# A graph layer on one core: the table of turned rows made in the set-up, and more chunks taken from it

## The chip, the cores and the metric

One Trainium2 chip, one of its cores. The time is device microseconds for one launch of the kernel; the median over runs counts. A profile is of one execution, and its span is the time between the first and last instruction on the engines. The engines are called PE (TensorE), DVE (VectorE), ACT (ScalarE), POOL (GpSimd) and SP (SyncE, which here mainly starts DMAs).

## The reference, cut to what matters

12500 nodes with 128 features each, and 200000 edges sorted by their target `dst`.

```python
h   = jnp.maximum(_layernorm(x, axis=-1), 0.0)
agg = jax.ops.segment_sum(h[src], dst, num_segments=12500)
deg = jax.ops.segment_sum(ones, dst, num_segments=12500)
agg = agg / jnp.maximum(deg, 1.0)[:, None]
t = jax.nn.relu(agg @ Wg + h @ Ws + bg)      # 128 -> 128
t = jnp.tanh(t @ W1 + b1)                    # 128 -> 512
t = jnp.tanh(t @ W2 + b2)                    # 512 -> 512
out = x + t @ W3 + b3                        # 512 -> 128
```

## The kernel before, in words

**Set-up.** The first 123 us. The rows of x come in 11 pieces of up to ten tiles of 128 nodes (the loop at L300). Each piece is normalised by `centre` (DVE, with a square on ACT), `factors` (a square root on ACT) and `scale` (DVE), and the result `h` is stored in a DRAM table `htab`, one row of 512 bytes for each node (L317). The indices are loaded and turned by `indices`. Meanwhile POOL gathers the source rows of 80 "raw" chunks straight from x (L179), which are normalised later.

**Chunks.** The 200000 edges make 1563 chunks of 128. For each chunk the 128 source rows have to be in SBUF, one edge to a partition; `add` (L643) multiplies them on PE with a one-hot matrix of the targets and adds to a PSUM tile of the node block (`agg`, or `edge` for chunks that reach over a block's border). The rows of a chunk come in one of these ways:

- POOL gathers them with one indirect DMA from `htab` (`gather`, L386), into a ring of 24 buffers (`AHEAD`). This is the usual way, 1323 chunks before.
- Lane 0: SP starts 128 DMAs of one row each, with addresses from registers (`row_loads`, L415).
- Lane 1: ACT copies 128 columns, one by one, out of `tab` (`column_copies`, L436). `tab` is the whole of `h` turned, features on the partitions and nodes along the free axis, and lies in SBUF. The column's place is in a register.
- Lane 2: DVE does the same two columns at a time (`column_pairs`, L446).

Columns have to be turned back: `turn` (L456) does that on PE, with one product for an ACT chunk and two for a DVE chunk, into a PSUM tile `pm`, and ACT copies it to SBUF as `turned`. The places come into registers with loads of 16 on ACT and DVE and of 32 on SP (`offsets`, L395; the loads are L399).

**Who gets which chunk.** `slots` (L126) is every fourth chunk from `FROM` on, without raw ones. A loop with debts (`owed`) deals the slots to the lanes in the proportions of `SHARES`, which counts the chunks of lanes 0, 1 and 2: 14, 50 and 96. What is left goes to POOL.

**Layers.** When the chunks of a block of 512 nodes are through, the five layer parts follow (`part0` to `part4`): products on PE, activations on ACT (L473), a last addition on DVE (L805), a store by SP. `part0` reads `tab` as well, for `h @ Ws`.

**Order.** PE, ACT and SP run in the order in which the program is written (`keep_in_program_order`; the classes `pe` and `act` and the function `sp_dma`). The main loop (L882) goes through the chunks: it issues gathers up to 24 ahead, lets the lanes' generators go on at times that `load_times` (L833) has worked out in advance, issues the turns nine gathered chunks ahead, and puts layer parts between the chunks by a planner's costs (1.251 us for each gathered chunk).

**The table.** `tab` is made while the first chunks run: `own` (L693) loads a block of `htab` back, 25 loads in all, and `own_turned` (L701) turns it on PE (98 transposes into `pt`) and has ACT copy it to `tab` (25 copies). The calls stand ahead of the main loop and at L941, one block to every second chunk. Columns can be taken only when the table is there; the first slot is above chunk 104.

Of the kernel before, what the change touches and what calls it, by code (L numbers as in the profile page):

```python
# [22 lines left out]
F32 = mybir.dt.float32  # L23
# [8 lines left out]
P = 128  # L32
EPS = 1e-5
CPR = 16
BLK = 512
# [9 lines left out]
SPREAD = 8  # L45
EVERY = 4
AT = 3
SHARES = 14, 50, 96
FROM, UNTIL = 104, 1540
SBUFS = 4  # L50
MARGIN = 18
TOGETHER = 4
# [25 lines left out]
def windowed(ctx, tc, x, src, dst, Wg, Ws, bg, W1, b1, W2, b2, W3, b3, out, flag):  # L78
    nc = tc.nc
    N, D = x.shape  # L80
# [18 lines left out]
    def raw(c):  # L99
        return RAW0 <= c < RAW1 and (c - RAW0) % STEP < GRP  # L100
# [23 lines left out]

    lanes = ([], [], [])
    slots = [c for c in range(AT, NCH, EVERY) if FROM <= c < UNTIL and not raw(c)]  # L126
    owed = [0.5 * n for n in SHARES] + [0.5 * (len(slots) - sum(SHARES))]
    for c in slots:
        owed = [o + n for o, n in zip(owed, [*SHARES, len(slots) - sum(SHARES)])]
        kind = max(range(4), key=lambda k: owed[k])  # L130
        owed[kind] -= len(slots)
        if kind < 3:
            lanes[kind].append(c)
    apart = sum(lanes, [])

    blocks, n = [], 0
# [16 lines left out]
    ps_t = ctx.enter_context(tc.tile_pool(name="ps_t", bufs=1, space=PSUM))  # L153
# [22 lines left out]
    for g in range(NRAW):  # L176
        t = raws.tile([P, GRP, D], F32, name=f"raw{g}")
# [7 lines left out]
    ident = const.tile([P, P], F32, name="ident")  # L185
# [5 lines left out]
    lane = shared[:, :W_MAX]  # L191
# [8 lines left out]
    htab = dram.tile([NP, D], F32, name="htab")  # L200
    bytes_at = dram.tile([ahead_of + NROW * ROW + past_end], U8, name="bytes_at")
    tab = const.tile([P, NP], F32, name="tab")
# [33 lines left out]
    def factors(stats):  # L236
        nc.scalar.activation(stats[:, 1], stats[:, 1], AF.Sqrt, bias=eps, scale=1.0 / D)
        nc.vector.reciprocal(stats[:, 1], stats[:, 1])

    def scale(h, xt, k, stats):  # L240
        nc.vector.scalar_tensor_tensor(h, xt, 0.0, spread(stats[:, 1], k), op0=ALU.max, op1=ALU.mult)  # L241

    with tc.tile_pool(name="ln", bufs=2) as ln:
# [53 lines left out]


        pieces = [(0, 4), (4, PIECE - 4)] + [(t, min(PIECE, NT - t)) for t in range(PIECE, NT, PIECE)]
        for i, (t0, k) in enumerate(pieces):  # L300
            xt = ln.tile([P, PIECE, D], F32, name="xt", bufs=3)
            whole = min(N - t0 * P, k * P) // P
            rest = min(N - t0 * P, k * P) - whole * P
            if rest:
                nc.vector.memset(xt[:, whole, :], 0.0)
            nc.sync.dma_start(xt[:, :whole, :], x[t0 * P : (t0 + whole) * P, :].rearrange("(t p) d -> p t d", p=P))
            if rest:
                nc.sync.dma_start(xt[:rest, whole, :], x[(t0 + whole) * P : N, :])
            if i == 1:
                indices("src", src, 0, keep_src)  # L310
            stats = ps_a.tile([P, BLK], F32, name="agg")[:, : 2 * k].rearrange("p (s t) -> p s t", s=2)
            xt = xt[:, :k]
            centre(ln, xt, k, stats)
            factors(stats)
            h = ln.tile([P, PIECE, D], F32, name="h", bufs=2)
            scale(h[:, :k], xt, k, stats)
            nc.sync.dma_start(htab[t0 * P : (t0 + k) * P, :].rearrange("(t p) d -> p t d", p=P), h[:, :k])  # L317


        number = sp.tile([NROW, CPR], F32, name="number")  # L320
# [50 lines left out]
    ml = ctx.enter_context(tc.tile_pool(name="ml", bufs=2))  # L371
# [11 lines left out]
    def sp_dma(*a):  # L383
        tc.keep_in_program_order(nc.sync.dma_start(*a))
# [93 lines left out]
    def raw_stats(i):  # L478
        return stats_raw[:, :, i * GRP : (i + 1) * GRP]

    def raw_scaled(i):
        h = raw_rows[i]
        scale(h, h, GRP, raw_stats(i))
        for j in range(GRP):
            rows_t[RAW0 + i * STEP + j] = h[:, j]
# [202 lines left out]
                s = out  # L688
            nc.vector.tensor_tensor(out, s, rd[:, a0 - n : a1 - n], op=ALU.mult)  # L689

    owns, xss, stores = {}, {}, []

    def own(s):  # L693

        n0 = s * BLK
        k = -(-min(BLK, N - n0) // P)
        hb = ml.tile([P, BLK // P, D], F32, name="xb")
        sp_dma(hb[:, :k], htab[n0 : n0 + k * P, :].rearrange("(t p) d -> p t d", p=P))
        owns[s] = hb

    def own_turned(s):  # L701

        k = -(-min(BLK, N - s * BLK) // P)
        hb = owns.pop(s)
        pt = ps_t.tile([P, BLK // P, P], F32, name="pt")
        for t in range(k):
            pe.transpose(pt[:, t, :], hb[:, t, :], ident)
        act.copy(tab[:, s * BLK : s * BLK + k * P], pt[:, :k, :].rearrange("p t n -> p (t n)"))

    def own_part(b):  # L710

# [121 lines left out]
    def load_times(lane):  # L833
        use = [sum(o < c for o in order) for c in lanes[lane]]
        if not use:
            return
        step = (use[-1] - use[0]) // max(1, len(use) - 1)
        use = [max(FROM - 46 + MARGIN, use[0] - step), *use] if lane else [use[0] - step * k for k in range(SBUFS - 1, 0, -1)] + use
        if lane == 0:
            use = [max(u, FROM // 2 + 7 * step // 8 * i) for i, u in enumerate(use)]  # L840
        some = LOADS[2] if lane == 2 else TOGETHER
        for i in range(len(lanes[lane])):
            for k in range(P // some):
                yield max(1, use[i] + (use[i + 1] - use[i]) * k * some // P - (0, MARGIN, MARGIN + GRP)[lane])
# [9 lines left out]
    def store(upto):  # L854
        while stores and stores[0][0] <= upto:
            sp_dma(*stores.pop(0)[1:])
# [11 lines left out]
            if w[1] is None:  # L868
                work.remove(w)

    nown = -(-N // BLK)
    own(0)
    own(1)
    own_turned(0)
    own(2)
    onehot(0)
    onehot(1)
    told_begins()
# [3 lines left out]
    for c in range(NCH):  # L882
        g = c // GRP
        at = c
        store(c if c >= QUICK else c - LATE)
        if c % GRP == 0 and g + 2 < ngrp:
            onehot(g + 2)
            if raw((g + 2) * GRP):
                raw_scaled(((g + 2) * GRP - RAW0) // STEP)
            if g == 2 + NRAW + 2:  # L890
                worst = checked()
            if 2 <= g < 2 + NRAW:
                centre(ed, raw_rows[g - 2], GRP, raw_stats(g - 2), bufs=1)
            if g == 2 + NRAW + 5:
                factors(stats_raw)

        if c % (GRP // 2) == 0 and g + 2 < ngrp:
            copies, times = loading[2]
            while times and times[0] <= behind:
                times.pop(0)  # L900
                next(copies, 0)
        while c % GRP == GRP // 2 and counted < len(blocks) and reach[counted][-1] // GRP <= g + (c >= QUICK):
            count(counted)
            counted += 1
        while nxt < len(order) and nxt < behind + AHEAD:
            gather(order[nxt])
            nxt += 1
        if not raw(c) and c not in apart:
            behind += 1
            for rows_of_lane, times in loading[:2]:  # L910
                while times and times[0] <= behind:
                    times.pop(0)
                    next(rows_of_lane, 0)
            while turns and turns[0][0] <= behind:
                turn(turns.pop(0)[1])
        if c >= QUICK:

            there = 7.5 + 1.251 * (NRAW * GRP + order.index(c)) if c not in apart else 0
            if c == QUICK:
                now = there - SPREAD  # L920
            while soonest() and max(now, soonest()[2]) < there:
                go_on(soonest())
            now = max(now, there) + 0.27
        add(c)

        lead = LEAD if c < QUICK else 2
        if done < len(blocks) and (c - lead if across[done] else c) >= reach[done][-1]:
            quick = reach[done][-1] + LEAD >= QUICK

            prev, older = (i if i >= 0 and reach[i][-1] + LEAD < QUICK else None for i in (done - 1, done - 2))  # L930
            older = None if quick and prev is None else older
            work.append([layers(done, prev, older), 0, 0, 0, quick and blocks[done][1] <= P])
            done += 1

        if c % TILE_EVERY == 1 and c // TILE_EVERY < NT:
            tallied(c // TILE_EVERY)
            if c // TILE_EVERY == NT - 1:
                outside(worst)
            if c // TILE_EVERY + EARLY < NT:
                seen(c // TILE_EVERY + EARLY)  # L940
        if c % 2 == 1 and c // 2 + 1 < nown:  # L941
            own_turned(c // 2 + 1)
            if c // 2 + 3 < nown:
                own(c // 2 + 3)
        if c < QUICK:
            if c % 2 == 0:
                go_on(work[0] if work else None)
        if c == QUICK:
            for b, (_, n) in enumerate(blocks):
                if n < BLK:  # L950
                    own_part(b)
# [376 lines left out]
```

## Time and profile before

| what | before |
|---|---|
| median of three runs | 2171.02 us |
| lowest, highest | 2165.9, 2172.37 us |
| profiled execution | 2164.96 us |
| its span | 2163.2 us |
| granted PE clock, mean of the span | 0.75 |
| HBM read, written | 123.71 MB, 13.03 MB |

How to read a profile row: a group of instructions is given as line, engine, operation, output <- inputs (partitions x elements), xcount, then the busy time in us, the mean duration of one in ns, and after the bar the idle time of the engine just before these instructions, with what ended most of it. "issue" is idle time in which the engine waited for nothing that the profile shows, "remote" time that ended by an event whose sender isn't shown. Durations of neighbours on one engine may overlap, so busy time can be less than count times mean. Rows that begin with a line and have three numbers with slashes give the minimum, median and maximum duration in ns, and the first and last start. Rows that begin with two numbers are of the timeline: start and length in us. A row that begins with a window gives the busy time of PE, its weight loads, DVE, ACT and POOL in it, then the granted clock, the share of the DMA engines' time, and GB/s. The line PEclk gives the granted clock of PE in 40 slices, in tenths. SPq, ACTq and DVEq are the sequencers of these engines, which do the register loads and issue DMAs.

### The profile page before, as it was taken

To read this page: it belongs to the slowest core of one execution; us is meant where nothing else is said; L and a number is where in the kernel's file an instruction comes from. 1 tells how busy PE (TensorE), PEld (TensorE's weight loads), DVE (VectorE), ACT (ScalarE), POOL (GpSimd) and SP (SyncE) were. 2 spreads that over 40 slices of the span, in tenths; PEclk is the share of its full clock that TensorE was granted. 3 is DMA by queue.
4 is the path that set the end of the run, shared out by engine and by line. 5 is a ranking of instruction groups with operands and counts; after the bars stand their busy time and mean duration, and the time that the engine had idled before them with its cause. 6 is when DMAs were issued, how large, how long until landed. Compare 5 with 4: busy or idle time off the path is not lost.

```text
span 2163.2 us, 34925 instructions
## 1 busy us (share of the span) xinstructions
PE 1474.7 (68%) x5402; PEld 981.4 (45%) x5402; DVE 1274.1 (59%) x7014; ACT 933.4 (43%) x6907; POOL 1335.4 (62%) x1411
## 2 busy tenths in 40 slices
PE   0025543768687787776885876767787687798587
PEld 0024433445454454454553544545454454454457
DVE  3854365756466675665673765666576476566530
ACT  1201144545544444454544445445454454545432
POOL 7756666566666666666666566666666666666661
PEclk9999985766866766776676776777766776788589
DMA  5934221222221222222222122122222122221210
GB/s 137 243 99 124 58 51 49 52 54 58 54 58 49 61 59 55 54 61 59 52 59 57 49 59 58 51 59 60 51 57 63 47 61 66 53 61 53 56 48 22
DMA packets 132962, 139.16 MB, mean 64 GB/s; under 512 B 31655, under 2 KB 109347, under 8 KB 132536
## 3 DMA queue, kind: packets, MB, share of 16 engines
q0 software_dynamic: 44896, 92.04, 16.7%
q1 hardware_dynamic: 84558, 41.29, 7.1%
q10 hardware_dynamic: 3276, 3.51, 0.6%
q14 instruction: 181, 1.48, 0.2%
q8 instruction: 51, 0.84, 0.2%
HBM read 123.71 MB, written 13.03 MB: 63 GB/s over the span
## 4 chain that ended last, share of the span: by engine, by line
PE 37%; DVE 20%; issue 17%; another core or an unknown queue 11%; ACT 9%; DVEq 2%; DMA 1%; ACTq 1%; SPq 0%
PE pm L378 24%; DVE cols L451 12%; PE agg L378 7%; ACT cols L442 7%; PE edge L378 3%; DVEq L399 2%; ACT h L473 2%; PE pt L381 1%; DVE nearby L535 1%; ACTq L399 1%; PE pm L381 1%; DVE mT L689 1%; DVE oh L495 1%; DVE h L241 1%
## 5 line engine op out<-in xcount | busy, mean ns | idle before, releaser
L388 POOL DMA_INDIRECT rows<-htab,scol x1323 | 1257.7, 951 | 759.7 <-issue 294.0
L451 DVE SCALAR_TENSOR_TENSOR cols<-first_only,tab 128x2 f32<-128x2 f32 x6144 | 913.8, 217 | 404.8 <-issue 394.7
L378 PE MATMUL pm<-h,w 128*128 128x512 f32 (+4 forms) x1344 | 836.1, 724 | 184.1 <-ACT h L473 66.8
L442 ACT COPY cols<-tab 128x1 f32 x6400 | 713.9, 188 | 489.1 <-issue 482.3
L378 PEld LDWEIGHTS agg<-oh,rows 128*128 128x128 f32 x1914 | 420.2, 275 | 285.1 <-issue 269.9
L378 PE MATMUL agg<-oh,rows 128*128 128x24 f32 x1914 | 382.1, 314 | 38.7 <-issue 35.0
L378 PEld LDWEIGHTS pm<-h,w 128*128 128x128 f32 x1344 | 253.7, 237 | 213.7 <-ACT h L473 71.6
L378 PEld LDWEIGHTS edge<-oh,rows 128*128 128x128 f32 x732 | 138.7, 238 | 96.1 <-issue 91.1
L473 ACT ACTIVATE h<-pm,b2c 128x512 f32<-128x512 f32 (+4 forms) x112 | 70.7, 631 | 173.7 <-PE pm L378 57.7
L378 PE MATMUL edge<-oh,rows 128*128 128x24 f32 x732 | 131.3, 286 | 17.6 <-issue 14.0
L805 DVE TENSOR_TENSOR o<-pt,xb 128x512 f32<-128x512 f32 x23 | 15.9, 692 | 203.9 <-remote 83.2
L495 DVE TENSOR_TENSOR oh<-shared,dloc 128x192 f32<-128x192 f32 x186 | 64.8, 350 | 86.2 <-remote 34.1
L473 ACT ACTIVATE h<-pm,b1c 128x512 f32<-128x512 f32 (+4 forms) x112 | 70.1, 631 | 99.5 <-remote 33.6
L476 ACT COPY turned<-pm 128x128 f32<-128x128 f32 x146 | 38.2, 262 | 158.2 <-PE agg L378 60.6
L378 PE MATMUL pm<-ident,cols 128*128 128x128 f32 x192 | 57.9, 394 | 54.8 <-ACT h L473 27.3
L179 POOL DMA_INDIRECT raw<-in_x_dram,rsrc x80 | 76.8, 960 | 25.6 <-issue 24.1
L535 DVE TENSOR_SCALAR_CACHE_REDUCE nearby<-nearby,parity 128x656 uint8<-128x656 uint8 x98 | 87.0, 887 | 6.1 <-issue 6.1
L285 PE MATMUL pm<-ident,idx_f 98*128 98x98 f32 x32 | 6.2, 376 | 108.4 <-DVE idx_f L279 68.5
L378 PEld LDWEIGHTS pm<-ident,cols 128*128 128x128 f32 x192 | 40.9, 257 | 71.3 <-ACT h L473 33.8
L378 PEld LDWEIGHTS agg<-oh,turned 128*128 128x128 f32 x194 | 47.2, 270 | 55.9 <-issue 35.0
L381 PE MATMUL pt<-ident,xb 128*128 128x128 f32 x98 | 27.1, 431 | 61.0 <-issue 32.8
L381 PE MATMUL pm<-ident,degs 128*128 128x128 f32 x99 | 24.9, 374 | 62.9 <-ACT h L473 30.3
(120 smaller groups left out, 808.3 us busy)
## 6 DMA issues: line engine op xcount, KB each, us to landing
srows<-htab SPq DMA_DIRECT2D x1792, 0.5 KB
rows<-htab,scol POOLq DMA_INDIRECT x1323
nearby<-bytes_at SPq DMA_DIRECT2D x98, 82.0 KB
xb<-htab SPq DMA_DIRECT2D x24, 256.0 KB
xb<-in_x_dram SPq DMA_DIRECT2D x23, 256.0 KB
out_dram<-o SPq DMA_DIRECT2D x23, 256.0 KB
xt<-in_x_dram SPq DMA_DIRECT2D x8, 640.0 KB
htab<-h SPq DMA_DIRECT2D x8, 640.0 KB
```

The costliest lines, as they stand in the source:

```text
L179: nc.gpsimd.indirect_dma_start(out=t[:, j, :], out_offset=None, in_=x, in_offset=bass.IndirectOffsetOnAxis(ap=rsrc[:, g, j : j + 1], axis=0),)
L241: nc.vector.scalar_tensor_tensor(h, xt, 0.0, spread(stats[:, 1], k), op0=ALU.max, op1=ALU.mult)
L378: tc.keep_in_program_order(nc.tensor.matmul(*a, **k))
L381: tc.keep_in_program_order(nc.tensor.transpose(*a, **k))
L388: nc.gpsimd.indirect_dma_start(out=r, out_offset=None, in_=htab, in_offset=bass.IndirectOffsetOnAxis(ap=scol[:, c : c + 1], axis=0),)
L399: loads, vs = nc.values_load_multi_w_load_instructions(places[min(lane, 1)][r : r + 1, q // EVERY, p0 : p0 + LOADS[lane]], engines=[kind], ...
L442: tc.keep_in_program_order(nc.scalar.copy(to[:, t : t + 1], of))
L451: last[:] = [tc.keep_in_program_order(nc.vector.scalar_tensor_tensor(to, first_only, a, b.to_broadcast([P, 2]), op0=ALU.mult, op1=ALU.add))]
L473: tc.keep_in_program_order(nc.scalar.activation(*a, **k))
L476: tc.keep_in_program_order(nc.scalar.copy(*a))
L495: newest[:] = [nc.vector.tensor_tensor(oh[:, :k, :w], lane[:, None, :w].to_broadcast([P, k, w]), dloc[:, g * GRP : g * GRP + k][:, :, None ...
L535: done = nc.vector.tensor_scalar(w, w, parity[:, t % 2 : t % 2 + 1], None, op0=ALU.is_equal, op1=ALU.add, accum_out=found[:, t : t + 1])
```

## The change

The table is no longer made from reloaded rows. A new `turned(h, t0, k)` in the set-up turns a normalised piece, up to four tiles at a time, on PE and copies it to `tab` on ACT; it is called for a piece after the `factors` of the next one, and after the loop for the last. `own`, `own_turned` and their calls are gone. Slots begin at chunk 27 (`FROM` = 24); lane 0 still begins after 104 (`ROWS_FROM`). The lanes get 24, 100 and 100 chunks, and the dealing loop uses shares in fractions, with lane 0's share over the later slots only. `load_times` begins lanes 1 and 2 one step ahead of their first use, with no lower bound from `FROM`; lane 0's bound uses `ROWS_FROM`, which leaves its value as it was.

By instruction, from the two built programs: ACT column copies 6400 to 12800, their register loads 400 to 800; DVE pairs 6144 to 6400, loads 768 to 800; SP row DMAs 1792 to 3072, loads 56 to 96, reloads of `htab` 25 to 0; gathers from `htab` 1323 to 1259; `turned` copies 146 to 200; `tab` copies 25 to 29.

```diff
@@ -45,8 +45,8 @@
 SPREAD = 8
 EVERY = 4
 AT = 3
-SHARES = 14, 50, 96
-FROM, UNTIL = 104, 1540
+SHARES = 24, 100, 100
+FROM, UNTIL, ROWS_FROM = 24, 1540, 104
 SBUFS = 4
 MARGIN = 18
 TOGETHER = 4
@@ -124,11 +124,13 @@
 
     lanes = ([], [], [])
     slots = [c for c in range(AT, NCH, EVERY) if FROM <= c < UNTIL and not raw(c)]
-    owed = [0.5 * n for n in SHARES] + [0.5 * (len(slots) - sum(SHARES))]
+    late = sum(c >= ROWS_FROM for c in slots)
+    owed = [0.5] * 4
     for c in slots:
-        owed = [o + n for o, n in zip(owed, [*SHARES, len(slots) - sum(SHARES)])]
+        shares = [SHARES[0] / late * (c >= ROWS_FROM), *(n / len(slots) for n in SHARES[1:])]
+        owed = [o + n for o, n in zip(owed, [*shares, 1 - sum(shares)])]
         kind = max(range(4), key=lambda k: owed[k])
-        owed[kind] -= len(slots)
+        owed[kind] -= 1
         if kind < 3:
             lanes[kind].append(c)
     apart = sum(lanes, [])
@@ -297,6 +299,17 @@
 
 
         pieces = [(0, 4), (4, PIECE - 4)] + [(t, min(PIECE, NT - t)) for t in range(PIECE, NT, PIECE)]
+        def turned(h, t0, k):
+            for s in range(0, k, 4):
+                m = min(4, k - s)
+                pt = ps_t.tile([P, BLK // P, P], F32, name="pt")
+                for t in range(m):
+                    nc.tensor.transpose(pt[:, t, :], h[:, s + t, :], ident)
+                nc.scalar.copy(
+                    tab[:, (t0 + s) * P : (t0 + s + m) * P], pt[:, :m, :].rearrange("p t n -> p (t n)")
+                )
+
+        unturned = []
         for i, (t0, k) in enumerate(pieces):
             xt = ln.tile([P, PIECE, D], F32, name="xt", bufs=3)
             whole = min(N - t0 * P, k * P) // P
@@ -312,9 +325,13 @@
             xt = xt[:, :k]
             centre(ln, xt, k, stats)
             factors(stats)
+            while unturned:
+                turned(*unturned.pop())
             h = ln.tile([P, PIECE, D], F32, name="h", bufs=2)
             scale(h[:, :k], xt, k, stats)
             nc.sync.dma_start(htab[t0 * P : (t0 + k) * P, :].rearrange("(t p) d -> p t d", p=P), h[:, :k])
+            unturned.append((h, t0, k))
+        turned(*unturned.pop())
 
 
         number = sp.tile([NROW, CPR], F32, name="number")
@@ -688,24 +705,7 @@
                 s = out
             nc.vector.tensor_tensor(out, s, rd[:, a0 - n : a1 - n], op=ALU.mult)
 
-    owns, xss, stores = {}, {}, []
-
-    def own(s):
-
-        n0 = s * BLK
-        k = -(-min(BLK, N - n0) // P)
-        hb = ml.tile([P, BLK // P, D], F32, name="xb")
-        sp_dma(hb[:, :k], htab[n0 : n0 + k * P, :].rearrange("(t p) d -> p t d", p=P))
-        owns[s] = hb
-
-    def own_turned(s):
-
-        k = -(-min(BLK, N - s * BLK) // P)
-        hb = owns.pop(s)
-        pt = ps_t.tile([P, BLK // P, P], F32, name="pt")
-        for t in range(k):
-            pe.transpose(pt[:, t, :], hb[:, t, :], ident)
-        act.copy(tab[:, s * BLK : s * BLK + k * P], pt[:, :k, :].rearrange("p t n -> p (t n)"))
+    xss, stores = {}, []
 
     def own_part(b):
 
@@ -835,9 +835,9 @@
         if not use:
             return
         step = (use[-1] - use[0]) // max(1, len(use) - 1)
-        use = [max(FROM - 46 + MARGIN, use[0] - step), *use] if lane else [use[0] - step * k for k in range(SBUFS - 1, 0, -1)] + use
+        use = [use[0] - step, *use] if lane else [use[0] - step * k for k in range(SBUFS - 1, 0, -1)] + use
         if lane == 0:
-            use = [max(u, FROM // 2 + 7 * step // 8 * i) for i, u in enumerate(use)]
+            use = [max(u, ROWS_FROM // 2 + 7 * step // 8 * i) for i, u in enumerate(use)]
         some = LOADS[2] if lane == 2 else TOGETHER
         for i in range(len(lanes[lane])):
             for k in range(P // some):
@@ -868,11 +868,6 @@
             if w[1] is None:
                 work.remove(w)
 
-    nown = -(-N // BLK)
-    own(0)
-    own(1)
-    own_turned(0)
-    own(2)
     onehot(0)
     onehot(1)
     told_begins()
@@ -938,10 +933,6 @@
                 outside(worst)
             if c // TILE_EVERY + EARLY < NT:
                 seen(c // TILE_EVERY + EARLY)
-        if c % 2 == 1 and c // 2 + 1 < nown:
-            own_turned(c // 2 + 1)
-            if c // 2 + 3 < nown:
-                own(c // 2 + 3)
         if c < QUICK:
             if c % 2 == 0:
                 go_on(work[0] if work else None)
```

## The prediction

> **What bounds the kernel now.** I read the totals, the granted clock, the chain of work that ended last, and the costliest groups.
>
> ```profile
> span 2163.2 us, 34925 instructions
> PE 1474.7 (68%) x5402; PEld 981.4 (45%) x5402; DVE 1274.1 (59%) x7014; ACT 933.4 (43%) x6907; POOL 1335.4 (62%) x1411
> PEclk9999985766866766776676776777766776788589
> ...
> PE 37%; DVE 20%; issue 17%; another core or an unknown queue 11%; ACT 9%; DVEq 2%; DMA 1%; ACTq 1%; SPq 0%
> ...
> L388 POOL DMA_INDIRECT rows<-htab,scol x1323 | 1257.7, 951 | 759.7 <-issue 294.0
> L451 DVE SCALAR_TENSOR_TENSOR cols<-first_only,tab 128x2 f32<-128x2 f32 x6144 | 913.8, 217 | 404.8 <-issue 394.7
> L378 PE MATMUL pm<-h,w 128*128 128x512 f32 (+4 forms) x1344 | 836.1, 724 | 184.1 <-ACT h L473 66.8
> L442 ACT COPY cols<-tab 128x1 f32 x6400 | 713.9, 188 | 489.1 <-issue 482.3
> ```
>
> No engine is full, and the chain passes from one to another: five engines feed one order of chunks. But the last two columns of L442 tell more than ACT's 43%. Its 6400 column copies are busy for 713.9 us, and the idle time just before them is 489.1 us, of which 482.3 us is "issue": the copy waited for no other engine. So copying takes ACT 713.9 + 489.1 = 1203.0 us, or 1203.0 / 6400 = 188 ns a copy. To see where that issue time lies, I read a stretch of the timeline on three engines (start, length, operation, idle before).
>
> ```profile
> 1036.87 2.31 ACT L442 COPY cols<-tab 128x1 f32 x24
> ...
> 1451.25 0.19 ACT L442 COPY cols<-tab 128x1 f32 x1 [0.54 <-issue]
> 1451.97 0.19 ACT L442 COPY cols<-tab 128x1 f32 x1 [0.53 <-issue]
> 1457.63 2.97 ACT L442 COPY cols<-tab 128x1 f32 x30 [0.46 <-issue]
> ```
>
> ```profile
> 1451.26 0.22 DVE L451 SCALAR_TENSOR_TENSOR cols<-first_only,tab 128x2 f32<-128x2 f32 x1 [0.51 <-issue]
> ...
> 1453.73 0.95 POOL L388 DMA_INDIRECT rows<-htab,scol  x1 [0.30 <-issue]
> 1454.98 0.94 POOL L388 DMA_INDIRECT rows<-htab,scol  x1 [0.30 <-issue]
> 1459.43 0.94 POOL L388 DMA_INDIRECT rows<-htab,scol  x1 [3.51 <-issue]
> ```
>
> Copies run either dense, 24 in 2.31 us (96 ns each), or in spells where ACT starts one each 1451.97 - 1451.25 = 0.72 us. In the spell DVE's pairs have the same gap before them, while POOL issues a gather each 1454.98 - 1453.73 = 1.25 us; in POOL's idle time before 1459.43, ACT copies 30 in a row. I take it that a spell comes with POOL gathering without a pause. This is an inference from a few places, and the size of the answer hangs on it.
>
> The next rows give the pace of gathers, of register loads, and everything else that ACT does from the first column copy to the end.
>
> ```profile
> L388 POOL DMA_INDIRECT rows<-htab,scol x1323: 942/947/1933, 123.2 to 2120.5; - x189
> L399 ACTq TENSOR_LOAD <-place x400: 1005/1044/1618, 252.3 to 2073.6; - x134
> L442 ACT COPY cols<-tab x6400: 176/188/205, 253.6 to 2083.4; 128x1 f32 x194
> ```
>
> ```profile
> L473 ACT ACTIVATE h<-pm,b2c 128x512 f32<-128x512 f32 (+4 forms) x112 | 70.7, 631 | 173.7 <-PE pm L378 57.7 <-PE agg L378 42.3 <-PE edge L378 37.4
> L473 ACT ACTIVATE h<-pm,b1c 128x512 f32<-128x512 f32 (+4 forms) x112 | 70.1, 631 | 99.5 <-remote 33.6 <-PE agg L378 33.4 <-PE pm L378 17.8
> L476 ACT COPY turned<-pm 128x128 f32<-128x128 f32 x146 | 38.2, 262 | 158.2 <-PE agg L378 60.6 <-remote 54.5 <-PE edge L378 19.9
> L473 ACT ACTIVATE h<-pm,b3c 128x512 f32<-128x512 f32 (+4 forms) x28 | 17.7, 631 | 31.1 <-remote 13.8 <-PE agg L378 10.4 <-PE pm L381 4.1
> L473 ACT ACTIVATE h<-pm,bgc 128x512 f32<-128x512 f32 (+4 forms) x28 | 17.6, 630 | 33.0 <-remote 19.8 <-PE pm L378 10.5 <-PE agg L378 1.4
> L476 ACT COPY sums<-edge 128x280 f32<-128x280 f32 (+5 forms) x26 | 9.7, 372 | 20.7 <-remote 9.2 <-PE agg L378 9.0 <-PE edge L378 1.8
> ```
>
> Their busy times add up to 224.0 us and their waits to 516.2 us. So from 253.6 us on ACT is filled by 1203.0 us of copying, 224.0 of other work and 516.2 of waiting. These make 253.6 + 1943.2 = 2196.8 us against a span of 2163.2; the account overshoots by 1.6%, which I don't correct. ACT's only slack is that waiting.
>
> **The change, part by part.** The instruction orders of the two programs give the counts.
>
> *ACT columns, 50 to 100 chunks.* 6400 more copies and 400 more register loads (each for 16 registers); 54 more copies `turned<-pm` in all, 50 of them for these chunks. All are on ACT in a fixed order, and MLP activations and `turned` copies stand behind them, so what ACT is late with, PE waits for. The price p of a copy, loads included, is the disputed number. Its low end is 96 ns; the high one is the mean of the rows, 188, with a stretch that went at
>
> ```profile
> L442 ACT COPY cols<-tab 128x1 f32 x5292 | 594.1, 189 | 431.7 <-issue 426.1
> L442 ACT COPY cols<-tab 128x1 f32 x1104 | 119.2, 188 | 57.4 <-issue 56.2
> ```
>
> (594.1 + 431.7) / 5292 = 194 ns from 253 to 1771 us, and (119.2 + 57.4) / 1104 = 160 ns from there to 2083 us, the end of the columns. At 188 ns the 6400 new copies cost 1203 us, at 96 they cost 614. I take **142 ns**, the middle: with ACT late, PE frees POOL's 24 row buffers later, POOL pauses more, and in its pauses the copies are dense; but 1259 gathers at 1.25 us still fill 1574 us.
>
> *First column.* The first column chunk moves from above 104 to 27, and the first copies stand right behind the last `tab` copy of the set-up. So ACT starts columns at about 125 us (the first gather, 123.2 us, marks the end of the set-up), not 253.6: some 128 us more room.
>
> *ACT's other terms.* Work: 224.0 + 54 x 0.262 = 238 us. Waits: those of 516.2 us that end with PE fall away when ACT itself is late. Bounds are 0 and 516; I take the part that ends with "remote", 33.6 + 54.5 + 13.8 + 19.8 + 9.2 = 130.9, and for the 54 new `turned` copies 54 x 54.5 / 146 = 20 more: 151 us.
>
> *The sum.* 125 + 12800 x 0.142 + 238 + 151 = **2332 us of span**, with ACT as the bound.
>
> *Register loads.* They are in p. The row has a median of 1.044 us for 16 registers, 65 ns each. The Trainium skill ("Runtime: NRT & Kernel Launch", section "Instruction fetch mechanics") gives some 200 ns for each register even in bulk, which speaks against the change: by it 800 loads of 16 would take 2560 us, an estimate from that page. The trace doesn't agree, and the measurement decides.
>
> *DVE pairs, 96 to 100 chunks.* 256 pairs x (913.8 + 404.8) / 6144 = 0.215 us: 55 us. DVE's idle time elsewhere covers it:
>
> ```profile
> L805 DVE TENSOR_TENSOR o<-pt,xb 128x512 f32<-128x512 f32 x23 | 15.9, 692 | 203.9 <-remote 83.2
> L495 DVE TENSOR_TENSOR oh<-shared,dloc 128x192 f32<-128x192 f32 x186 | 64.8, 350 | 86.2 <-remote 34.1
> ```
>
> 203.9 + 86.2 us of it stand before two groups alone. Without this cover it is +55; I take 0.
>
> *SP rows, 14 to 24 chunks, and the reloads.* 1280 more row DMAs and 40 more register loads; 25 reloads of 256 KB go. The rows share SP's queue with `nearby` loads, `xb` loads and stores.
>
> ```profile
> L384 SPq MOVE srows<-htab x1792: 2/29/1392, 222.6 to 1795.5; - x200
> L384 SPq DMA_DIRECT2D srows<-htab x1792: 3/197/1387, 222.7 to 1795.5; - x200
> 1435.35 17.32 SPq L384 DMA_DIRECT2D srows<-htab  x24
> ```
>
> At the medians a row takes SP 0.029 + 0.197 = 0.226 us: +289 us on a queue that now gives a row each (1795.5 - 222.6) / 1792 = 0.88 us. I take 0 on the path; in a spell, 24 rows in 17.32 us, 0.72 each, it is a rival.
>
> *POOL.* 64 gathers go: 64 x (2120.5 - 123.2) / 1323 = 64 x 1.510 = 97 us less, which counts only if POOL sets the pace.
>
> *PE.* 50 more ACT chunks with one turn and four more DVE ones with two: 58 small products at about
>
> ```profile
> L378 PE MATMUL pm<-ident,cols 128*128 128x128 f32 x192 | 57.9, 394 | 54.8 <-ACT h L473 27.3
> ```
>
> 0.4 us, 23 us; covered by PE's waits for ACT.
>
> *The table.* Before, it was made beside the first chunks:
>
> ```profile
> L476 ACT COPY tab<-pt x25: 372/586/586, 127.0 to 223.4; 128x512 f32<-128x512 f32 x24, 128x256 f32<-128x256 f32 x1
> L381 PE MATMUL pt<-ident,xb 128*128 128x128 f32 x98 | 27.1, 431 | 61.0 <-issue 32.8 <-DMA xb<-htab 15.0 <-ACT tab L476 13.0
> ```
>
> Gone are 25 loads, 98 transposes and 25 copies from between 127.0 and 223.4 us; PE waited 15.0 us for the loads. Since the pace there is POOL's gathers, that saves 0 to 15 us. In the set-up stand the same 98 transposes and 29 copies, one piece late, with one PSUM buffer. Fully exposed, a group of four takes 4 x 0.431 = 1.72 us, so 29 x 1.72 = 50 us, since ACT's next `sqrt` queues behind the copy, and `scale` and the store of `htab` behind that. PE and ACT are mostly idle in the set-up, so I take 2 us for it and 2 saved: 0. Both ends stay in the range.
>
> **From span to time.** The profiled execution took 2164.96 us, 1.8 more than its span; the median of the three runs is 2171.02, 6.1 above it. 2332 + 1.8 + 6.1 = **2340 us**.
>
> **Rivals.**
>
> *A, the other side: ACT absorbs the columns and the gathers set the pace.* For it speaks that gathering now runs steadily from 123.2 to 2120.5 us, and that ACT gains 128 us of room. Then the span is 123.2 + 1259 x 1.510 + (2163.2 - 2120.5) = 2067, or 2075 us as a median. It decides where 125 + 12800p + 238 + 151 falls under 2067: p below 121 ns. Break-even with 2163.2 is p = 129. Against it: even the late stretch, with little on SP, took 160 ns.
>
> *B, the price stays.* If spells don't thin out, p is 160 to 194 ns: the span is 514 + 12800p, 2562 to 2997; at 175 ns, 2754 us, 2762 as a median. For it speak the rows; against it, that POOL must then stand still for over a third of the time, and it is in such pauses that copies go dense.
>
> *C, SP's rows set the pace.* 3072 rows at 0.72 us from 222.6 us end at 2434; with about the 90 us that now follow the last ACT load (2163.2 - 2073.6) that is 2524, 2532 as a median. Against it: most rows take 0.226 us.
>
> *D, a slow clock.* PE starves while it waits for `turned`, and its products slow down.
>
> ```profile
> 253.00:2083.00 1830.00, 1342.34 (x4691) 863.11 (x4691) 1128.21 (x6759) 877.10 (x6795) 1141.14 (x1205) 0.71 0.22 56
> 1028.40 2.08 PE L378 MATMUL pm<-h,w 128*128 128x512 f32 x2 [3.73 <-issue]
> 1018.07 1.10 PE L378 MATMUL pm<-h,w 128*128 128x512 f32 x2
> ```
>
> The first row is the main stage: PE busy 1342.34 us at a granted clock of 0.71. Two products took 2.08 us after a pause of 3.73 us and 1.10 us elsewhere. At half clock throughout, PE would be busy 1342.34 x 0.71 / 0.5 = 1906 us; with 253 us before and 80 after, 2239, or 2247 as a median. The Trainium skill ("TensorE: Matmul & The Clock Gate", "Part 1: The HAM clock gate (the "warmup" mystery)") has the clock at half or full speed by how busy PE has lately been; the two rows agree.
>
> That the change doesn't do what it says is excluded: the built order holds 12800 copies, no reload, and the transposes in the set-up.
>
> **How the numbers follow.** Forecast (ACT bounds, p between 121 and 160) 0.54, A 0.25, B 0.13, C 0.04, D 0.04. The predicted time is the forecast's, 2340; its own range, by p from 129 to 160, is 2171 to 2570. The range of 8 in 10 has to reach A's 2075 and, below it, 20 us for the table and DVE's part: 2055. Upwards it takes C and the lower part of B, to p = 165: 514 + 2112 + 8 = 2634, so 2640. About 0.1 of B lies above and 0.05 below 2055, with 0.05 for the unforeseen. Changes under 0.3% can't be told from none. Faster: A and 0.02 of the forecast (p under 129), 0.27; within 0.3%: 0.03; slower: 0.70.
>
> **What would show it.** Right: L442 with x12800 and (busy + idle) / 12800 near 142 ns; few waits left before L473 and `turned`; a long POOL idle ended by PE; PE's `pm` and adds waiting for ACT. A: gathers still 1.5 us apart, last one near 2025 us, copies near 100 ns. B: p at 160 or more. C: adds waiting for `srows`. D: a granted clock near 0.5. The table: the first gather later than 123.2 us, and the stretch from 123 to 253 us. I am wrong above all if the spells aren't POOL's doing, or if ACT's waits for PE stay.

## The result, and the profile after

The changed kernel takes 2506.86 us (median of 4 runs, 2499.85 to 2517.79) against 2168.46 us for the kernel before (here over four runs, the three of the table above and one more): **1.157 times** as long, with a 95% interval of 1.151 to 1.162. The forecast was 2340 us, the range 2055 to 2640. The profiled execution has a span of 2500.3 us at a granted clock of 0.726.

One thing is needed to read the experiments. They ran in three groups, each on one chip with the kernel before beside it, and the chips differ: before took 2194 us beside acts50, acts75, rows14 and table_only, 2164 us beside old_table_100, half_gathers, fixed_columns and one_load, and 1784 us beside the last four, which fell on a third chip. So ratios are compared, and of the third chip only with each other. Each chip had one group only: that the chip makes the difference is taken from this, not shown.

The page of the changed kernel, with the lines that answer to those of before:

```profile
span 2500.3 us, 44616 instructions
PE 1539.4 (62%) x5468; PEld 1009.9 (40%) x5468; DVE 1305.6 (52%) x7270; ACT 1580.2 (63%) x13365; POOL 1273.5 (51%) x1347
...
L459 ACT COPY cols<-tab 128x1 f32 x12800 | 1376.5, 188 | 690.7 <-issue 675.0
L405 POOL DMA_INDIRECT rows<-htab,scol x1259 | 1195.6, 950 | 1160.7 <-PE agg L395 545.0
L468 DVE SCALAR_TENSOR_TENSOR cols<-first_only,tab 128x2 f32<-128x2 f32 x6400 | 937.6, 218 | 409.8 <-issue 402.5
L395 PE MATMUL pm<-h,w 128*128 128x512 f32 (+4 forms) x1344 | 873.0, 752 | 239.7 <-ACT h L490 111.0
```

(L459 is L442 of before, L405 is L388, L468 is L451, L395 is L378, L490 is L473, L493 is L476.) ACT's copies now take 1376.5 + 690.7 = 2067.2 us of 2500.3, and all but 16 us of their idle time is "issue", with another engine named for 0.8 us. POOL's idle time before its gathers has grown from 759.7 to 1160.7 us, 732 us of it ended by PE, 545.0 of them by the adds to `agg`: the row buffers come free late. PE in turn waits for ACT, by the waits of PE:

```profile
PE pm L395 <- ACT h L490: 245.1, 51, 14.9
PE pm L395 <- ACT turned L493: 132.1, 28, 16.5
PE agg L395 <- ACT turned L493: 72.7, 9, 21.8
```

Columns are total us, times and the longest. The rest of ACT's work hardly waits any more, by the groups on ACT from 140 us on:

```profile
L490 ACT ACTIVATE h<-pm,b2c 128x512 f32<-128x512 f32 (+4 forms) x112 | 70.0, 627 | 40.0 <-PE pm L395 28.2 <-issue 6.3 <-PE edge L395 5.3
L490 ACT ACTIVATE h<-pm,b1c 128x512 f32<-128x512 f32 (+4 forms) x112 | 69.3, 629 | 22.5 <-PE pm L395 17.9 <-issue 3.7 <-remote 0.5
L493 ACT COPY turned<-pm 128x128 f32<-128x128 f32 x200 | 51.5, 257 | 18.3 <-issue 7.7 <-PE pm L395 5.8 <-PE edge L395 4.6
L490 ACT ACTIVATE h<-pm,b3c 128x512 f32<-128x512 f32 (+4 forms) x28 | 17.6, 627 | 6.4 <-PE pm L395 6.1 <-issue 0.3
L490 ACT ACTIVATE h<-pm,bgc 128x512 f32<-128x512 f32 (+4 forms) x28 | 17.4, 626 | 4.0 <-PE pm L395 3.9
L493 ACT COPY sums<-edge 128x280 f32<-128x280 f32 (+5 forms) x27 | 10.0, 371 | 3.3 <-issue 3.1 <-PE edge L395 0.2
```

Busy 235.8 us, waiting 94.5 us, where before it waited 516.2. And the set-up ends later; the first start of gathers and of copies, by line:

```profile
L405 POOL DMA_INDIRECT rows<-htab,scol x1259: 942/947/2009, 160.1 to 2459.6; - x180
...
L459 ACT COPY cols<-tab x12800: 174/187/206, 160.4 to 2425.3; 128x1 f32 x197
```

Gathers begin at 160.1 us, not at 123.2.

### The profile page after: what moved, and what is told of

It reads as the page before. It is cut to its first block, busy times and chain, and to the rows that moved or that the text cites. A ratio compares the mean times of both kernels' runs of the same rounds, so it can differ in the third digit from the quotient of the medians.

```text
span 2500.3 us, 44616 instructions
## 1 busy us (share of the span) xinstructions
PE 1539.4 (62%) x5468; PEld 1009.9 (40%) x5468; DVE 1305.6 (52%) x7270; ACT 1580.2 (63%) x13365; POOL 1273.5 (51%) x1347
## 5 line engine op out<-in xcount | busy, mean ns | idle before, releaser
L459 ACT COPY cols<-tab 128x1 f32 x12800 | 1376.5, 188 | 690.7 <-issue 675.0
L405 POOL DMA_INDIRECT rows<-htab,scol x1259 | 1195.6, 950 | 1160.7 <-PE agg L395 545.0
L468 DVE SCALAR_TENSOR_TENSOR cols<-first_only,tab 128x2 f32<-128x2 f32 x6400 | 937.6, 218 | 409.8 <-issue 402.5
L395 PE MATMUL pm<-h,w 128*128 128x512 f32 (+4 forms) x1344 | 873.0, 752 | 239.7 <-ACT h L490 111.0
L395 PEld LDWEIGHTS agg<-oh,rows 128*128 128x128 f32 x1824 | 405.9, 281 | 283.2 <-issue 255.0
L395 PE MATMUL agg<-oh,rows 128*128 128x24 f32 x1824 | 366.9, 320 | 29.2 <-DMA rows<-htab,scol 15.5
L395 PEld LDWEIGHTS pm<-h,w 128*128 128x128 f32 x1344 | 262.2, 245 | 261.9 <-ACT h L490 115.9
L395 PE MATMUL pm<-ident,cols 128*128 128x128 f32 x200 | 67.1, 431 | 208.2 <-ACT h L490 134.0
L395 PEld LDWEIGHTS edge<-oh,rows 128*128 128x128 f32 x694 | 134.1, 242 | 88.1 <-issue 85.0
L395 PEld LDWEIGHTS pm<-ident,cols 128*128 128x128 f32 x200 | 44.3, 273 | 219.5 <-ACT h L490 140.3
L395 PE MATMUL edge<-oh,rows 128*128 128x24 f32 x694 | 123.3, 288 | 3.9 <-issue 2.1
L395 PEld LDWEIGHTS agg<-oh,turned 128*128 128x128 f32 x272 | 65.6, 269 | 143.9 <-ACT turned L493 74.7
L395 PE MATMUL agg<-oh,turned 128*128 128x24 f32 x272 | 60.9, 307 | 91.0 <-ACT turned L493 72.7
L307 PE MATMUL pt<-ident,h 128*128 128x128 f32 x98 | 28.3, 435 | 120.6 <-DVE h L243 55.3
L490 ACT ACTIVATE h<-pm,b2c 128x512 f32<-128x512 f32 (+4 forms) x112 | 70.0, 627 | 40.0 <-PE pm L395 28.2
L395 PE MATMUL pm<-tab,ws 128*128 128x512 f32 (+4 forms) x56 | 40.5, 815 | 81.8 <-ACT turned L493 65.7
L490 ACT ACTIVATE h<-pm,b1c 128x512 f32<-128x512 f32 (+4 forms) x112 | 69.3, 629 | 22.5 <-PE pm L395 17.9
L398 PE MATMUL pm<-ident,cols 128*128 128x128 f32 x100 | 36.8, 368 | 68.6 <-issue 18.5
```

The costliest lines, as they stand in the source:

```text
L307: nc.tensor.transpose(pt[:, t, :], h[:, s + t, :], ident)
L395: tc.keep_in_program_order(nc.tensor.matmul(*a, **k))
L398: tc.keep_in_program_order(nc.tensor.transpose(*a, **k))
L405: nc.gpsimd.indirect_dma_start(out=r, out_offset=None, in_=htab, in_offset=bass.IndirectOffsetOnAxis(ap=scol[:, c : c + 1], axis=0),)
L459: tc.keep_in_program_order(nc.scalar.copy(to[:, t : t + 1], of))
L468: last[:] = [tc.keep_in_program_order(nc.vector.scalar_tensor_tensor(to, first_only, a, b.to_broadcast([P, 2]), op0=ALU.mult, op1=ALU.add))]
```

## The experiments

Theory 1 after the result: ACT's copies set the end, with 0.1615 us each (2067.2 / 12800). Its rivals: the early columns, the table in the set-up, SP's rows.

**acts50**, ACT's share alone put back:

```diff
-SHARES = 24, 100, 100
+SHARES = 24, 50, 100
```

> The changed kernel with ACT's share put back from 100 to 50 chunks; all else of the change stays. Theory 1 (ACT's column copies set the end: 160.4 us until they begin, 12800 copies at 0.1615 us, about 236 us of other work, little waiting): with 6400 copies ACT needs well under 1900 us, so the old pace of the gathers returns, 14 gathers fewer at 1.51 us and a set-up that ends 37 us later: 2170 to 2200 us. Rival (the early columns, the table in the set-up or the rows on SP cost the time): it stays above 2400 us.

Measured: 2504.5 us, 1.144 times before (1.138 to 1.151). Theory 1 missed badly. ACT is idle again; the profile names another wait:

```profile
L459 ACT COPY cols<-tab 128x1 f32 x6400 | 703.3, 188 | 478.1 <-issue 469.2
...
L552 DVE TENSOR_SCALAR_CACHE_REDUCE nearby<-nearby,parity 128x656 uint8<-128x656 uint8 x98 | 87.5, 893 | 539.8 <-DMA nearby<-bytes_at 491.0
```

DVE stands 491.0 us for its `nearby` loads, and its `mT` and column pairs, which stand behind them, are late for PE, by the waits of PE:

```profile
PE pm L395 <- DVE mT L706: 158.8, 21, 19.5
...
PE pm L395 <- DVE cols L468: 88.4, 12, 19.0
```

The loads are issued by SP, in this order (timeline of SP, then the row DMAs by line):

```profile
1200.56 16.55 SPq L401 DMA_DIRECT2D srows<-htab  x27
1217.86 0.01 SPq L401 DMA_DIRECT2D nearby<-bytes_at  x1
1217.89 25.31 SPq L401 DMA_DIRECT2D srows<-htab  x44
1243.36 0.36 SPq L401 DMA_DIRECT2D nearby<-bytes_at  x1
```

```profile
L401 SPq DMA_DIRECT2D srows<-htab x3072: 2/228/1390, 245.8 to 2288.1; - x192
```

SP's queue is filled with rows, at (2288.1 - 245.8) / 3072 = 0.665 us each over the whole, and a `nearby` load stands behind 27 or 44 of them. So there seemed to be **two bounds of nearly one height**, ACT's copies and SP's rows: theory 2.

**acts75**, ACT's share at 75 (`SHARES = 24, 75, 100`).

> The changed kernel with 75 chunks for ACT. Theory 1 (ACT is the bound only beyond a point): 160 + 9600 x 0.165 + 222 + 95 less some 50 of overlap is about 2010 us, below the gathers' pace, so 2170 to 2250 us, and the slope from 50 to 75 chunks is much smaller than from 75 to 100. Rival (each column chunk has its price on the path whatever the number): halfway between 50 and 100 chunks, about 2340 us.

Measured: 2464.81 us, 1.123 times (1.116 to 1.129); neither the 2170 to 2250 of theory 1 nor the straight line's 2340. DVE's wait for `nearby` is there again, and with it SP's queue; the row is of the waits of DVE:

```profile
DVE nearby L552 <- DMA nearby<-bytes_at: 439.1, 51, 23.0
```

With 25 chunks more on ACT than acts50 it is faster; 25 gathers fewer fit that, but this wasn't taken apart.

**rows14**, SP's share alone put back:

```diff
-SHARES = 24, 100, 100
+SHARES = 14, 100, 100
```

> The changed kernel with SP's share put back from 24 to 14 chunks. Theory 1 (ACT is the bound): 2490 to 2525 us, no difference that matters. Rival (SP's row DMAs hold up the chunks, 0.23 to 0.72 us a row): faster by up to 10 x 128 x 0.23 = 290 us or more.

Measured: 2536.4 us, 1.156 times (1.149 to 1.162). With SP relieved nothing is won: `nearby` waits for no load any more, and ACT holds the end, by the chain of rows14:

```profile
ACT 47%; issue 27%; PE 13%; DVE 4%; another core or an unknown queue 4%; ACTq 4%; DMA 0%; SPq 0%; DVEq 0%
...
L459 ACT COPY cols<-tab 128x1 f32 x12800 | 1377.5, 188 | 701.0 <-issue 683.9
```

**old_table_100**, the kernel before with ACT's share alone raised:

```diff
-SHARES = 14, 50, 96
+SHARES = 14, 100, 96
```

> The kernel before with ACT's share alone raised from 50 to 100 chunks; the table from reloads, columns from above chunk 104. Theory 1 (ACT works without a break from its first column to the end): columns begin at about 250 us instead of 160, so 250 + 12800 x 0.1615 + 236 + 95 less 58 of overlap, about 2590 us, slower than the changed kernel by some 90 us. Rival (another part of the change makes it slow): near 2170 us. Second rival (the beginning doesn't matter): as the changed kernel, 2507 us.

Measured: 2488.4 us, 1.151 times (1.147 to 1.154). So 50 more chunks on ACT are enough for all of the slowdown. They cost less than expected here:

```profile
L442 ACT COPY cols<-tab 128x1 f32 x12800 | 1363.7, 188 | 591.8 <-issue 577.1
```

(1363.7 + 591.8) / 12800 = 153 ns a copy, though the copies begin 96 us later, at 256.7 us and not at 160.4. The second rival of this run holds: the early start is worth nothing that shows.

**table_only**, the kernel before with the table in the set-up:

```diff
-SHARES = 24, 100, 100
-FROM, UNTIL, ROWS_FROM = 24, 1540, 104
+SHARES = 14, 50, 96
+FROM, UNTIL, ROWS_FROM = 104, 1540, 104
```

> The kernel before with the table made in the set-up and nothing else of the change: shares 14, 50 and 96, slots from chunk 104. Theory 1: the set-up ends 37 us later as in the changed kernel, and the stretch of the first chunks gets back a part of it, at most the 15 us that PE waited for the reloads and some of the 61 us before the transposes: 2175 to 2205 us. Rival, as the prediction took it: no cost, 2160 to 2172 us.

Measured: 2240.02 us, 1.023 times (1.017 to 1.028), some 46 us slower than before on that chip. It costs more than either theory had. The gathers show where most of it lies: they start 38.6 us later than 123.2. (When the last one starts can't be compared, as the profile of before is of an execution of 2164.96 us and this chip's took 2194.)

```profile
L405 POOL DMA_INDIRECT rows<-htab,scol x1323: 939/946/1957, 161.8 to 2192.3; - x189
...
L308 ACT COPY tab<-pt x29: 372/586/586, 24.6 to 160.7; 128x512 f32<-128x512 f32 x20, 128x256 f32<-128x256 f32 x9
```

The next three ask what makes a copy dear.

**half_gathers**, every second gather left out:

```diff
+    twice = []
+
     def gather(c):
+        if order.index(c) % 2:
+            rows_t[c] = twice[0]
+            return
         r = rows_in.tile([P, D], F32, name="rows")
+        twice[:] = [r]
```

> The changed kernel with every second gather of POOL left out: two chunks in a row use the same gathered rows, so half of the gathered rows are not those of the reference; all copies, rows, products and layers stay. Theory 1a (the idle time 'issue' before ACT's copies, 675 us in the changed kernel, comes from POOL gathering without a pause): it falls below 340 us, a copy costs 0.13 us or less instead of 0.1615, and the span is about 2070 us. Rival (the issue time belongs to the 800 register loads of ACT, 1.04 us each, 830 us in all): issue stays above 600 us, a copy at 0.16, the span at 2450 to 2500.

Measured, one run: 1913.85 us, span 1911.7.

```profile
L465 ACT COPY cols<-tab 128x1 f32 x12800 | 1295.5, 188 | 139.3 <-issue 123.5
...
L411 POOL DMA_INDIRECT rows<-htab,scol x630 | 600.3, 953 | 1140.7 <-PE agg L395 780.8
```

Issue time falls from 675.0 to 123.5 us, and a copy costs (1295.5 + 139.3) / 12800 = 112 ns. So POOL's gathers make ACT's copies dear; whether it is POOL's issuing of them or the transfer of the rows isn't told apart, as both were halved. The span is some 160 us below the 2070 that was expected. SP's 3072 rows go faster too, from 226.4 to 1708.3 us, 0.48 us each.

**fixed_columns**, ACT copies 12800 fixed columns, with no registers:

```diff
+            by_pair = columns[c].rearrange("p (t i) -> p i t", t=2)
             for p0 in range(0, P, LOADS[1]):
-                for p, to, *ab in two(1, c, p0):
-                    for t, of in enumerate(ab):
-                        tc.keep_in_program_order(nc.scalar.copy(to[:, t : t + 1], of))
+                for p in range(p0, p0 + LOADS[1], 2):
+                    for t in range(2):
+                        tc.keep_in_program_order(nc.scalar.copy(by_pair[:, p // 2, t : t + 1], tab[:, 96 * p + t : 96 * p + t + 1]))
```

> The changed kernel with ACT's copies taken from fixed columns of the table, without register loads and register offsets: 100 chunks get wrong source rows, the number of copies is the same. Theory 1a (POOL's gathers slow whatever ACT starts): issue time before the copies stays above 500 us and the span above 2350 us. Rival (loads or register offsets are the price): a copy costs about 0.1 us, issue time is under 150 us, ACT is no longer the bound and the span comes to 2100 to 2200 us.

**one_load**, register loads once a chunk, the registers used eight times:

```diff
+            vs = None
             for p0 in range(0, P, LOADS[1]):
-                for p, to, *ab in two(1, c, p0):
-                    for t, of in enumerate(ab):
-                        tc.keep_in_program_order(nc.scalar.copy(to[:, t : t + 1], of))
+                if vs is None:
+                    vs = [v for _, v in offsets(1, c, p0)]
+                by_pair = columns[c].rearrange("p (t i) -> p i t", t=2)
+                for p in range(p0, p0 + LOADS[1], 2):
+                    for t in range(2):
+                        of = tab[:, bass.ds((vs[p - p0 + t] - TAB_AT) // 4, 1)]
+                        tc.keep_in_program_order(nc.scalar.copy(by_pair[:, p // 2, t : t + 1], of))
```

> The changed kernel with one register load of 16 places for each of ACT's chunks instead of eight, the 16 places used eight times over: 100 chunks repeat 16 source rows; all 12800 copies keep their register offsets. Theory 1a (POOL's gathers): issue time above 550 us, span 2400 to 2500 us. Rival (the register loads): issue time under 250 us, span 2100 to 2200 us.

Measured, one run each: 2482.47 and 2473.2 us, with these rows in the one and in the other:

```profile
L460 ACT COPY cols<-tab 128x1 f32<-128x1 f32 x12800 | 1347.7, 192 | 674.8 <-issue 669.0
```

```profile
L464 ACT COPY cols<-tab 128x1 f32 x12800 | 1343.3, 189 | 677.1 <-issue 670.7
```

Issue time stays at 669.0 and 670.7 us: neither the register loads nor the register offsets are the price. Copies from fixed places are held up as much. These two ran on the chip of half_gathers, so that its 123.5 us stands against about 670 there.

The last four were to settle SP's part, and ran on the third chip.

**rows24**, the kernel before with SP's share alone raised (`SHARES = 24, 50, 96`).

> The kernel before with SP's share alone raised from 14 to 24 chunks. Theory 2 (SP is a second bound: with 24 chunks its queue runs without a break at about 0.65 us a row while POOL gathers, as it did in acts50 from 245.8 to 2288.1 us): 222 + 3072 x 0.65 + about 200 us from the last row to the end, 2350 to 2500 us, with DVE's nearby waiting for its loads as in acts50. Rival (SP has room, and acts50 was slow from the early columns or the table): 2140 to 2190 us.

**both_back**, the changed kernel with both shares put back (`SHARES = 14, 50, 100`).

> The changed kernel with both shares put back, 14 chunks for SP and 50 for ACT; the table in the set-up, the columns from chunk 27 and 100 chunks for DVE stay. Theory 2 (ACT's copies and SP's rows are two bounds, each near 2500 us by itself, so that undoing one shows nothing): as table_only, 1.00 to 1.03 times the kernel before. Rival (a third cause, the early columns): above 1.10 times.

**cols60**, the kernel before with 60 chunks for ACT (`SHARES = 14, 60, 96`).

> The kernel before with 60 chunks for ACT, not 50. Theory 1 (ACT's load costs nothing until it is the bound): 250 + 7680 x 0.17 + 230 is about 1790 us, so ACT isn't the bound, and 10 gathers fewer give up to 15 us: 0.99 to 1.005 times the kernel before. Rival (each ACT chunk costs its share of the 324 us that 50 more did in old_table_100): 65 us slower, 1.03 times.

**table_raw_later**, table_only with the raw gathers issued from the main loop.

> The kernel of table_only with POOL's 80 gathers of raw rows moved from the start of the set-up to the first ten groups of the main loop. Theory 3 (in the set-up the table's groups each waited up to 10 us because POOL gathered without a pause until 103 us): the set-up, read as the start of the first gather from htab, ends by 125 us, not at 162. Rival (the hand-overs between PE and ACT cost it by themselves, 29 groups at about 1.8 us, 52 us in all): it still ends after 145 us. The time as a whole: 80 more gathers in the main stage against an earlier start, 2190 to 2290 us.

Measured, as ratios to before on that chip (1784.27 us): rows24 0.993 (0.992 to 0.995), both_back 0.995 (0.994 to 0.997), cols60 0.993 (0.991 to 0.994), table_raw_later 0.999 (0.998 to 1.000). On this chip spells hardly exist. Of rows24, a row of the page, the gathers and SP's rows by line, and two gathers from the timeline:

```profile
L442 ACT COPY cols<-tab 128x1 f32 x6400 | 650.8, 188 | 80.3 <-issue 71.6
```

```profile
L388 POOL DMA_INDIRECT rows<-htab,scol x1313: 940/944/1922, 107.2 to 1751.2; - x188
...
L384 SPq DMA_DIRECT2D srows<-htab x3072: 227/228/353, 171.1 to 1573.1; - x192
```

```profile
1005.34 0.94 POOL L388 DMA_INDIRECT rows<-htab,scol  x1 [0.30 <-issue]
1006.59 0.95 POOL L388 DMA_INDIRECT rows<-htab,scol  x1 [0.30 <-DMA rows<-htab,scol]
```

POOL gathers each 1.25 us from 107.2 to 1751.2 us, (1751.2 - 107.2) / 1313 = 1.252 us, and that is the whole main stage; ACT's copies cost (650.8 + 80.3) / 6400 = 114 ns beside it, and SP's rows, of which one takes at most 0.353 us to issue, (1573.1 - 171.1) / 3072 = 0.456 us. Ten gathers fewer are 12.5 us, and rows24 and cols60 are 13 and 14 us faster than before. So here the gathers are the bound, and theory 2, which is on chips with spells, is left open. table_raw_later says nothing on theory 3: its raw gathers still ran first, from 3.0 to 105.6 us, as in table_only. So it shows what table_only does on this chip, 0.999 times, and with both_back that the table in the set-up is free here. In both_back's timeline the transposes follow each other, where in the changed kernel they stood still:

```profile
55.50 1.11 PE L307 MATMUL pt<-ident,h 128*128 128x128 f32 x4 [1.38 <-ACT tab L308]
57.29 1.12 PE L307 MATMUL pt<-ident,h 128*128 128x128 f32 x4 [0.68 <-ACT tab L308]
59.08 0.69 PE L307 MATMUL pt<-ident,h 128*128 128x128 f32 x2 [0.68 <-ACT tab L308]
```

```profile
68.83 1.11 PE L307 MATMUL pt<-ident,h 128*128 128x128 f32 x4 [4.00 <-issue]
79.54 1.12 PE L307 MATMUL pt<-ident,h 128*128 128x128 f32 x4 [9.60 <-issue]
90.75 0.69 PE L307 MATMUL pt<-ident,h 128*128 128x128 f32 x2 [10.10 <-issue]
```

Both stretches lie in POOL's raw gathers; the first is both_back, the second the changed kernel. A group each 1.8 us there, one each 5 to 11 us here. The last raw gather of the changed kernel starts at 103.3 us, and from 116.62 us on its groups too follow each other:

```profile
116.62 1.11 PE L307 MATMUL pt<-ident,h 128*128 128x128 f32 x4 [1.39 <-ACT tab L308]
118.41 1.12 PE L307 MATMUL pt<-ident,h 128*128 128x128 f32 x4 [0.68 <-ACT tab L308]
```

That the raw gathers make them stand still is read from this; no run took those gathers away. both_back's gathers from `htab` begin at 107.1 us, rows24's, with the old table, at 107.2.

## Why the prediction held, point by point

**ACT becomes the bound: right.** old_table_100 shows it with that part alone, rows14 with SP's part taken out. The signs named came: x12800, few waits left on ACT (94.5 us, 516.2 before), POOL's idle ended by PE (545.0 us), PE waiting for ACT. The size was not right: the slowdown is 338 us, twice the 2340 - 2171 = 169 of the forecast.

**The price of a copy: mis-sized.** "I take 142 ns, the middle" failed; the changed kernel has 161.5. 12800 x 0.0195 = 250 us too little. The other terms: start 160.4 for 125, +35; work 235.8 for 238, -2; waits 94.5 for 151, -57; and the account overshoots, as it did for before, here by 160.4 + 2067.2 + 235.8 + 94.5 - 2500.3 = 57.6 us. 250 + 35 - 2 - 57 - 58 = 168 us, the difference between 2332 and 2500.3. The waits and the overshoot took back 115 us of the error, by luck. The stretch at 160 ns, quoted as the lower end of rival B, would have been the better row, but why isn't shown: POOL is busy 63% of it and 62% of the stretch at 194 ns (196.92 of 312 us, 944.22 of 1518), so its pauses don't tell the two apart; in the changed kernel it is 51% (1113.34 of 2172 us from 253 us on).

**The reason for the price: right in kind.** That POOL's gathering makes the spells was an inference; half_gathers shows it on a chip with spells (123.5 us, where fixed_columns and one_load have about 670), and these two exclude registers. The trace of the changed kernel bears it out as a whole: sorted by the middle of the idle time before them, 3141 of the 12800 copies stand where POOL had gathered for over 2 us without a pause of 0.45 us, and before these ACT idled 450.5 of the 690.7 us; 2283 stand where POOL had paused for over 2 us, with 9.9 us. (The Trainium skill, "Runtime: NRT & Kernel Launch", section "Instruction fetch mechanics", has a register load at some 200 ns a register. That page speaks of loads from HBM, while the places here lie in SBUF. With all loads the issue time was 675.0 us, with one of eight left 670.7, with none 669.0, so that here the loads lie hidden.) But it isn't the whole cause: on the third chip POOL gathered without any pause and there were no spells. What the chips differ in, no run shows.

**SP's rows at 0 on the path: doubtful.** Rival C, at 0.04, gave a span of 2524 us; acts50 has 2492.9, SP's queue full and DVE waiting 491.0 us behind it. In the changed kernel the same wait is short, by the waits of DVE:

```profile
DVE nearby L552 <- DMA nearby<-bytes_at: 23.9, 3, 11.2
```

Theory 2 explains it so: ACT is as late as SP, the two bounds lie side by side, and undoing one shows nothing. It isn't shown; it is read from the profile and from the gap between acts50 (1.144) and table_only (1.023) on one chip, which also holds the early columns and four more DVE chunks; raising SP's share alone wasn't tried on a chip with spells.

**The table at 0: wrong.** "PE and ACT are mostly idle in the set-up, so I take 2 us" failed. It costs 37 to 39 us of set-up and 1.023 in all alone. Idle engines didn't help: a hand-over between PE and ACT took up to 10 us while POOL gathered raw rows on that chip. The bound of 50 us held, by luck: it was worked out from other durations, and it took all 29 groups as of four products where 9 have two, 98 x 0.431 = 42 us. In the time of the changed kernel the table doesn't show: old_table_100, without it, is 1.151 times before, and the changed kernel 1.157.

**128 us more room from early columns: useless.** It was 93 us (253.6 to 160.4), and old_table_100 without it is no slower.

**A, B, C, D.** A didn't happen here. On the third chip gathers do set the pace, so there it might; the changed kernel wasn't run there. B happened by its sign, p at 160 or more, if barely (161.5); its formula gives 514 + 12800 x 0.1615 = 2581 us of span there, 81 more than measured, and the spells did thin out, from 188 ns on average to 161.5. C's sign, adds waiting for `srows`, isn't among the waits of PE; whether SP's rows are a second bound is open, as said. D is out: the clock is 0.726.

## What to carry to other kernels

Before moving work to an engine that looks half idle, count its "issue" time with the work: ACT's 43% busy was (1203.0 + 224.0) / (2163.2 - 253.6) = 75% taken from the first column on, and doubling the copies filled it. When undoing one part of a slow change shows nothing, look for a second bound of the same height before giving the first one up; the waits of the run with one bound taken away name the other, and only a run with both taken away, on the same chip, proves it. And don't take the middle between the mean and the best case for the price of an instruction: ask of each stretch what the other engines did in it, and let the range cover the price of the dear ones.

## What was not expected of the hardware

On the chips with spells POOL's gathers held up what other engines started. With half of them gone, the issue time before ACT's copies was 123.5 us and not 675.0, before DVE's pairs 266.7 and not 402.5, and a row of SP took 0.48 us, not 0.65; in a spell ACT started one copy each 0.72 us. In the set-up PE and ACT stood for up to 10 us at a hand-over while raw rows were gathered. On the third chip little of it is seen: ACT's issue time before 6400 copies was 482.3 us in the kernel before and 71.6 us in rows24 there, which has ten more chunks on SP, and the kernel before took 1784 us, not 2168. A choice of shares tuned on the one chip may then not be the choice for the other: 60 chunks on ACT gained 0.7% there, and weren't tried on a chip with spells.
